# A two-layer graph transformer on one core: the same instruction steps in another written-out order

## The chip, the cores and the metric

The kernel runs on one core of one Trainium2 chip. The metric is the device time of one execution, in microseconds, as the median over runs. The engines are named as in the profile: PE is TensorE (PEld its weight loads), DVE is VectorE, ACT is ScalarE, POOL is GpSimd, SP is SyncE, whose queue issues nearly all DMAs.

## The reference, cut to what matters

Two layers run over 128 graphs of 128 nodes with 256 features, all in float32. `adj` is a 0/1 matrix per graph.

```python
# layer 0: attention over relations, then a feed-forward block
q, k = heads(src @ Wq + bq), heads(src @ Wk + bk)          # 8 heads of 32
attn = softmax(q @ k.T / sqrt(32))
out  = sum(attn * (adj == r) @ heads(src @ Wv[r] + bv[r]) for r in range(4))
x    = ln(src + out @ Wo + bo, g1, beta1)
x    = ln(x + gelu(x @ W1 + b1) @ W2 + b2, g2, beta2)      # 256 -> 1024 -> 256
# layer 1: two graph-attention steps, then a second feed-forward block
h = gat(gat(x, adj, W1, a1), adj, W2, a2)   # softmax over leaky_relu(Wh1 + Wh2.T) where adj > 0
h = ln(x + h, g_ln1, b_ln1)
return ln(h + relu(h @ w_ff1 + b_ff1) @ w_ff2 + b_ff2, g_ln2, b_ln2)
```

## The kernel before, in words

**Tiling.** The tokens are cut into 32 groups of four graphs (512 tokens). `fast_pass` (L190) carries each group through all stages; everything of three or four neighbouring groups runs interleaved. The weights stay in SBUF. A general path for other values of `adj` follows behind a flag and isn't run here.

**Stages.** Each stage is a Python generator, and each `yield` ends a step:

- `q`, `projected` (L744): q, k and v. The products of four blocks are made with seven half-size products instead of eight (a Strassen-Winograd form), in two PSUM banks (pqqa and pqqb, then pvqa and pvqb), with copies on ACT (L809, L806) and adds on DVE (L819, L831, L835, L804) between.
- `a`, `attention` (L959): for each pair p of graphs, scores `ps` on 32-row tiles of the array (L859), four exponentials `e` on ACT (L866), the mask on DVE (L875), then `pav` (L929) and `pden` (L917) on 32-column tiles, the normalisation (L941 to L956) and the output product `pwo` (L969).
- `d`, `folded` (L881): folds of e for the sums, four DMAs `es` by SP (L891), copies on ACT (L900), adds on DVE (L902).
- `f` and `fc`, `k` and `kc`: the two feed-forward blocks, both by `ffn` (L509). `f` and `k` are `others()` (L575), which works in the banks `ph1`/`po1` and `ph7`/`po7`; `fc` and `kc` are `chain()` (L619), which works in one bank, `seeded`. Here too seven half-size products replace eight. `product` (L521) issues two matmuls of 128x128 by 128x256, `product2` (L530) eight of 128x128 by 128x128.
- `l`, `layer1` (L1038): the two graph-attention steps, with `pw` (L1046), `py` (L1059) and `pg` (L1072), the spreading of a column over all partitions through HBM (two DMAs, L1008 and L1009) and `edges` (L1012) on ACT (L1017, L1023) and DVE.
- `n0` to `n3`, `norm` (L474): layer norms on DVE (L445), with the power -1/2 on POOL (L431); then the planes on ACT (L465) and a DMA transpose (L468). `t0` to `t2`, `turned` (L486): the copies of the transposed planes on ACT (L493), and the sums `yS` on DVE (L502 to L506).
- `in`, `rest`, `bo`, `out`, and the setup steps (`Lqk`, `wqk`, ...): loads, stores, prepared weights.

**The chain in `seeded`.** For each half r of a feed-forward block, `chain()` copies ph1 into `seeded` on ACT (L621, or L648 for the second half), adds the product T2 (yS), copies the bank out on ACT (L629, p16), adds the product T1, adds the bank to the hidden layer on DVE (L633), and adds the product B22. Each product on `seeded` waits for the step that read the bank before it.

**What sets the order.** Nothing is scheduled by the framework: engines take their instructions in the order in which Python issues them, and that order is written out in three strings, FRONT (L123), STEADY (L144) and TAIL (L159). `in_order` (L1163) reads tokens `name:group*times` and advances that stage's generator by one step each time; a group number is relative to the loop's. FRONT runs once, STEADY for g = 1 to 29, TAIL once. A step issues everything up to its next `yield`, on whichever engines it uses, DMAs on SP's queue included. Semaphore waits are added by the framework from the data that instructions share.

Of the kernel before, what the change touches and what calls it, by code (L numbers as in the profile page):

```python
# [120 lines left out]


FRONT = """  # L123
Lqk*2 in:0 q:0*2 L1 q:0 Lqk Lv Lqk wqk q:0*4 Lv q:0 a:0 Lv a:0*2 Lv L2 L1 a:0*2 rest:0 L1 Lv_ a:0
Lv_ L1 d:0*2 Lv_ q:0 a:0 q:0 w1 d:0*2 rest:0 L3 in:1 d:0*2 Lh1 Lo q:0*2 d:0 a:0 q:0 d:0 L1 q:0*2
a:0*2 q:0 a:0 wv a:0 w1 a:0*2 L1 a:0*6 d:0 bo:0 rest:1 d:0 w1 q:1*2 Lh1 d:0*2 q:1 Lg1 a:0 Lg1 L4
a:0 Lg1 q:1 d:0 bo:0 Lg1 q:1 d:0 q:1 Lg2 q:1 d:0 q:1 a:1 a:0 a:1 Lgat a:1 wqk d:0 a:1*2 a:0 a:1
a:0 d:1*2 a:1 a:0*4 Lgat L2 d:1 a:0*2 q:1 a:0 d:1*2 L3 q:1 a:0 b1 d:1 a:0 a:1 L2 bo:0 q:1 d:1
a:0*2 n0:0 q:1 b1 L2 n0:0 b1 output_bias q:1 d:1 a:1 n0:0*3 w2 n0:0 L4 b1 output_bias q:1 n0:0 w2
w1 Lgat a:1*2 Lh1 a:1 t0:0 gw f:0 a:1 b1 a:1 t0:0 Lgat a:1 q:1 t0:0*2 a:1 d:1 rest:1 a:1 fc:0 d:1  # L130
a:1 L4 t0:0 b1 d:1 f:0*2 q:1 t0:0 f:0 fc:0 a:1 d:1 L3 gw b1 a:1 fc:0 b1 f:0 fc:0 d:1 fc:0 d:1
a:1*2 f:0 L3 f:0 a:1 in:2 d:1*2 fc:0 a:1 f:0 w2 Lh1 w2 fc:0*2 gw f:0 fc:0*2 f:0 a:1*3 L3 fc:0*2
a:1 bo:1 fc:0 f:0 wv f:0 fc:0 f:0*2 fc:0 f:0 a:1 L4 fc:0*2 a:1*3 rest:2 u2 fc:0 a:1 fc:0 bo:1 a:1
f:0 fc:0 a:1 fc:0*2 f:0 a:1 f:0 fc:0 f:0 n0:1 Lg2 fc:0 n0:1 fc:0 n0:1*2 f:0 fc:0 n0:1 q:2 f:0 wqk
fc:0*2 q:2 L3 n0:1 fc:0 n0:1 f:0*2 gw t0:1 wqk fc:0 bo:1 f:0 fc:0 t0:1 gelu fc:0 n1:0 t0:1 n1:0
gw q:2*2 c1 q:2 t0:1 n1:0 c1 n1:0 f:1 q:2*2 n1:0 t0:1 q:2 t0:1 fc:1 n1:0 c1 n1:0 q:2*2 f:1 t1:0
q:2 fc:1 u2 t1:0 l:0 f:1 fc:1 l:0 t1:0 l:0 fc:1 t1:0 l:0 fc:1 l:0 u1 l:0*3 fc:1 f:1 l:0 f:1 q:2
f:1*2 fc:1 f:1 fc:1*2 q:2 f:1 fc:1*2 q:2*2 c1 exp q:2 wv fc:1 c1 q:2 c1 l:0*2 c1 l:0 fc:1 l:0*2
u2 q:2 l:0*2 fc:1 l:0 a:2 f:1 a:2*3 d:2 l:0 a:2 fc:1 l:0*2 a:2 l:0 d:2 l:0*3 u2 l:0 d:2 l:0*3 f:1
u1 q:2 l:0 u1 d:2 fc:1 f:1 Lh2 q:2 fc:1 q:2 f:1 a:2 f:1 q:2 Lh2 wv fc:1*2 f:1 u1 c1 d:2 f:1 l:0*2  # L140
fc:1 f:1 l:0*2 a:2 q:2 fc:1 l:0*2 fc:1 l:0*2 fc:1 l:0*3 f:1 q:2*2 d:2 fc:1 d:2 q:2 l:0 f:1 fc:1
l:0*3 q:2 l:0*2 n2:0 q:2 rest:2 f:1 fc:1 n2:0*2 q:2 n2:0*2 fc:1*3 d:2
"""
# [36 lines left out]


# [1352 lines left out]
```

## Time and profile before

| | before |
|---|---|
| median of 3 runs | 2634.33 us (2633.99 to 2634.73) |
| profiled execution | 2633.71 us |
| its span, first to last instruction | 2631.9 us |
| PE / PEld busy | 2598.8 / 2302.5 us |
| DVE / ACT / POOL busy | 2246.7 / 1857.4 / 141.8 us |
| mean granted PE clock | 0.998 |
| start of FFN1 of group 1 / 2 / 3 / 30 | 101.5 / 193.1 / 274.1 / 2440.6 us |
| most groups from there to the next | 80.13 us |

A line of the timeline has the start in us, the time in us, the engine, the line of the kernel, the operation, the tile written and those read, the shapes, and how many instructions were merged; in brackets is the idle time before it and what ended it. One float32 matmul shows as two passes on PE, each with a weight load on PEld, so a `product` is four records and a `product2` sixteen. Ends of matmuls are modelled, so the spacing of starts is what to read: 0.216 us from pass to pass of 256 columns, 0.112 us for 128 columns. With PE busy for 99% of the span, what can change without changing the work is in the spacings that are longer than these.

### The profile page before, as it was taken

What the parts mean: (1) busy time and instruction counts of PE and PEld (TensorE: products, weight loads), DVE (VectorE), ACT (ScalarE), POOL (GpSimd) and SP (SyncE); (2) the same over time, 40 slices, a digit from 0 to 9 for tenths busy, and PEclk for the clock granted to TensorE, in tenths of its full rate; (3) what the DMA queues carried; (4) which work ended last, traced back from release to release, by engine and by line L of the source; (5) the groups of instructions that cost most, each with busy time, mean ns of one, the idle gap of its engine ahead of it and who ended that gap; (6) DMA issues with size and microseconds to landing.
All of it is one profiled execution on the core that took longest, in us unless ns stands there. A gap on an engine that the chain in (4) does not pass through costs nothing.

```text
span 2631.9 us, 54467 instructions
## 1 busy us (share of the span) xinstructions
PE 2598.8 (99%) x20842; PEld 2302.5 (87%) x20842; DVE 2246.7 (85%) x5921; ACT 1857.4 (71%) x3839; POOL 141.8 (5%) x137
## 2 busy tenths in 40 slices
PE   8999999999999999999999999999999999999997
PEld 6888898888988988988889888889889899888886
DVE  5888888889888988888988888988889888889877
ACT  4767777667677677776776776776767777767764
POOL 0000000000000000000000000000000000000000
PEclk9999999999999999999999999999999999999999
DMA  6222232232233222222322232222323222222211
GB/s 177 69 63 61 64 66 66 53 73 65 55 67 61 65 61 65 65 66 53 75 64 59 63 67 59 63 64 65 69 53 73 61 61 65 65 57 70 60 29 34
DMA packets 317371, 170.60 MB, mean 65 GB/s; under 512 B 222768, under 2 KB 295600, under 8 KB 317104
## 3 DMA queue, kind: packets, MB, share of 16 engines
q1 hardware_dynamic: 316000, 166.66, 28.0%
q8 instruction: 166, 2.72, 0.4%
q14 instruction: 101, 0.83, 0.1%
q10 hardware_dynamic: 1104, 0.40, 0.1%
HBM read 66.20 MB, written 16.90 MB: 32 GB/s over the span
## 4 chain that ended last, share of the span: by engine, by line
PE 92%; DVE 3%; DMA 2%; ACT 2%; issue 1%; SPq 0%; POOL 0%; ACTq 0%; POOLq 0%; DVEq 0%
PE po L534 16%; PE ph L525 16%; PE seeded L525 13%; PE seeded L534 12%; PE pwo L969 4%; PE pav L929 4%; PE pw L1046 4%; PE pqqa L789 4%; PE pvqa L789 4%; PE pqqb L789 3%; PE pvqb L789 3%; PE ps L859 2%; PE py L1059 2%; PE pg L1072 2%; PE pden L917 1%; DVE x L445 1%
## 5 line engine op out<-in xcount | busy, mean ns | idle before, releaser
L465 ACT COPY planes<-x 128x512 uint16<-128x512 uint16 x384 | 227.0, 617 | 161.2 <-DVE x L445 160.5
L493 ACT COPY yT<-pT 128x512 uint16<-128x512 uint16 x384 | 268.0, 764 | 63.6 <-DMA pT<-planes 63.6
L431 POOL TENSOR_TENSOR rs<-rs,mhalf 128x4 f32<-128x4 f32 x129 | 139.5, 1081 | 2430.7 <-DVE rs L430 1836.9
L525 PE MATMUL seeded<-yS,w_L_gnn_w_ff 128*128 128x256 f32 x768 | 208.8, 394 | 2.8 <-ACT seeded L621 1.6
L866 ACT ACTIVATE e<-ps 128x512 f32<-128x512 f32 x256 | 137.0, 591 | 103.1 <-issue 89.9
L525 PE MATMUL seeded<-yS,w_L_gnn_W 128*128 128x256 f32 x768 | 204.0, 388 | 1.3 <-DVE yS L505 0.9
L525 PE MATMUL ph<-yT,w_L_gnn_w_ff 128*128 128x256 f32 x768 | 201.1, 385 | 0.5 <-ACT yT L493 0.2
L525 PE MATMUL ph<-yT,w_L_gnn_W 128*128 128x256 f32 x768 | 197.1, 380 | 0.0
L407 DVE BATCH_NORM_STATS2 st<-x 128x6 f32<-128x256 f32 x512 | 190.8, 414 | 2.4
L534 PE MATMUL po<-w_L_gnn_W,hT 128*128 128x128 f32 x1536 | 187.1, 275 | 0.5 <-ACT hT L549 0.5
L534 PEld LDWEIGHTS po<-w_L_gnn_W,hT 128*128 128x128 f32 x1536 | 184.0, 192 | 3.8 <-ACT hT L549 0.6
L534 PE MATMUL po<-w_L_gnn_w_ff,hT 128*128 128x128 f32 x1536 | 186.9, 275 | 0.0
L534 PEld LDWEIGHTS po<-w_L_gnn_w_ff,hT 128*128 128x128 f32 x1536 | 183.8, 192 | 3.4
L525 PEld LDWEIGHTS seeded<-yS,w_L_gnn_w_ff 128*128 128x128 f32 x768 | 135.7, 189 | 51.3 <-ACT p L629 16.1
L875 DVE TENSOR_TENSOR pm<-e,adj 128x512 f32<-128x512 f32 x256 | 169.7, 683 | 10.3 <-ACT e L866 9.2
L525 PEld LDWEIGHTS seeded<-yS,w_L_gnn_W 128*128 128x128 f32 x768 | 140.4, 190 | 35.2 <-ACT p L629 8.3
L633 DVE TENSOR_TENSOR hT<-seeded,p 128x512 f32<-128x512 f32 x128 | 87.6, 684 | 90.6 <-PE seeded L525 87.1
L525 PEld LDWEIGHTS ph<-yT,w_L_gnn_w_ff 128*128 128x128 f32 x768 | 143.7, 191 | 23.3 <-ACT seeded L648 0.6
L525 PEld LDWEIGHTS ph<-yT,w_L_gnn_W 128*128 128x128 f32 x768 | 143.3, 190 | 18.8 <-ACT seeded L621 0.4
L900 ACT COPY pm<-e 64x512 f32<-64x512 f32 x256 | 157.6, 616 | 2.3
L629 ACT COPY p<-seeded 128x512 f32<-128x512 f32 x128 | 75.0, 586 | 97.0 <-PE seeded L525 96.7
L549 ACT ACTIVATE hT<-hT,c_L_gnn_b_ff 128x256 f32<-128x256 f32 x256 | 112.4, 498 | 34.5 <-DVE hT L633 32.3
(195 smaller groups left out, 6399.2 us busy)
## 6 DMA issues: line engine op xcount, KB each, us to landing
es<-e SPq DMA_DIRECT2D x256, 128.0 KB, 2.4
xT<-in_xT_dram SPq DMA_DIRECT2D x32, 512.0 KB, 3.9
x<-in_x_dram SPq DMA_DIRECT2D x32, 512.0 KB, 3.9
out_dram<-x SPq DMA_DIRECT2D x31, 512.0 KB, 2.9
spread<-hbm SPq DMA_DIRECT2D x61, 256.0 KB, 4.1
adj<-in_adjT_dram SPq DMA_DIRECT2D x32, 256.0 KB, 4.4
pT<-planes SPq DMA_TRANSPOSE x192, 3.1
w_L_gnn_W<-in_L_gnn_W_dram SPq DMA_DIRECT2D x8, 256.0 KB, 5.1
```

What stands on the lines that cost most here:

```text
L407: nc.vector.bn_stats(st[:, b % 2, :], S["x"][:, b, :])
L431: nc.gpsimd.tensor_tensor(rs[:, bs], rs[:, bs], k.mhalf[:, bs], op=ALU.pow)
L465: nc.scalar.copy(planes[:, :, b], words)
L493: nc.scalar.copy(o.rearrange("p (b t h) -> p h b t", b=2, h=2), pT[:, :, :, c, :])
L525: nc.tensor.matmul(bank[:, s * TH : (s + 1) * TH], wa[:, form, 0, f * P : (f + 1) * P], m, start=start and s == 0, stop=True, skip_group_c ...
L534: nc.tensor.matmul(bank[:, s * P : (s + 1) * P], m[:, f, s * P : (s + 1) * P], wb_[:, form, f, :], start=start and s + f == 0, stop=True, ...
L549: nc.scalar.activation(o[:, s], o[:, s] if src is None else src[:, s * TH : (s + 1) * TH], func, bias=ba[:, f : f + 1],)
L789: nc.tensor.matmul(bank[:, s * TH : (s + 1) * TH], *ops, start=start and s == 0, stop=True, skip_group_check=True,)
L866: nc.scalar.activation(e[:, s], pss[s], AF.Exp, scale=SCALE)
L875: nc.vector.tensor_mul(pm[:, s], S["e", p][:, s], S["ad"][:, pair(p), None, :].to_broadcast([P, 2, NCH, P]),)
L900: nc.scalar.copy(ea[own], e[own, hs, lo].rearrange("p s c i -> p s (c i)"))
L929: nc.tensor.matmul(pav[s * DH : (s + 1) * DH, u, c, :], v[:, d0 : d0 + DH], m[:, s, u, c, :], start=(r == 0), stop=(r == 1),)
```

## The change

Only the three strings differ. The set of steps is the same (FRONT has 486 steps before and 526 after, STEADY 291 and 291, TAIL 449 and 409), every instruction of the old program is in the new one, and the order among the steps of a stage stays. What moves is the interleaving of stages on every engine, and where the period of STEADY is cut: its first step is `f:0` before and `k:-1` after. The string STEADY in full, of FRONT and TAIL their first and last lines:

```diff
 FRONT = """
-Lqk*2 in:0 q:0*2 L1 q:0 Lqk Lv Lqk wqk q:0*4 Lv q:0 a:0 Lv a:0*2 Lv L2 L1 a:0*2 rest:0 L1 Lv_ a:0
-Lv_ L1 d:0*2 Lv_ q:0 a:0 q:0 w1 d:0*2 rest:0 L3 in:1 d:0*2 Lh1 Lo q:0*2 d:0 a:0 q:0 d:0 L1 q:0*2
...
+Lg1 Lqk in:0 Lqk q:0 Lqk L1 q:0 Lqk q:0*4 rest:0 q:0 Lv*3 Lv_ q:0 a:0 L1 a:0*2 Lv a:0 L1 Lv_ a:0
+L1 Lg2 L1 d:0 Lv_ d:0 q:0 a:0 q:0*2 Lh1 d:0 a:0 d:0 q:0 d:0*2 L2 d:0 w1 a:0 d:0 a:0 q:0 w1 q:0*2
...
 STEADY = """
-f:0*2 a:1 f:0 q:1*3 n2:-1*2 t2:-1 fc:0 a:1 t2:-1*2 a:1*2 t2:-1 f:0 fc:0 k:-1 t2:-1 a:1 t2:-1 fc:0
-k:-1 a:1 kc:-1 a:1*3 n1:0 d:1 kc:-1*2 a:1 n1:0 d:1 k:-1 d:1 a:1 d:1 a:1*3 k:-1*2 kc:-1*2 d:1*3
-k:-1 n1:0 k:-1 a:1 d:1 n1:0 kc:-1 a:1 n1:0 k:-1 kc:-1 bo:1 kc:-1 k:-1*2 n1:0 a:1 k:-1 a:1*4
-kc:-1*4 n1:0 a:1*2 in:2 kc:-1 a:1 bo:1 kc:-1 k:-1 a:1 t1:0 k:-1 kc:-1 t1:0 k:-1 t1:0 a:1 kc:-1*2
-k:-1 l:0*2 kc:-1 l:0 t1:0 k:-1 l:0 a:1 l:0*2 a:1 kc:-1 l:0*2 n0:1 kc:-1 n0:1 bo:1 l:0 k:-1 kc:-1
-q:2 n0:1 kc:-1*2 n0:1 rest:2 k:-1 q:2 n0:1*2 l:0*2 kc:-1 l:0*2 k:-1*2 kc:-1 q:2 k:-1 q:2 kc:-1
-l:0 n0:1 l:0 kc:-1 q:2 gelu kc:-1*2 l:0 t0:1 l:0 k:-1 kc:-1 l:0 t0:1 l:0*2 t0:1 k:-1 t0:1 f:1 l:0
-kc:-1 l:0 t0:1*2 q:2*2 k:-1 q:2 l:0 fc:1 f:1 l:0 fc:1*2 kc:-1 f:1 l:0 f:1 q:2 l:0 q:2 n3:-1 fc:1
-l:0 f:1 l:0 f:1 fc:1 l:0 fc:1*2 f:1*2 fc:1*2 n3:-1 q:2 n3:-1 fc:1 f:1 fc:1*2 f:1 fc:1 out:-1
-f:1*2 fc:1 q:2 rest:2 f:1 fc:1*2 l:0 f:1 l:0 q:2 l:0 fc:1*2 l:0 q:2 f:1 q:2 fc:1 l:0 q:2 f:1 q:2
-fc:1*2 f:1 q:2 l:0 a:2 fc:1 l:0 a:2 l:0 f:1 a:2 exp q:2 l:0*2 a:2 l:0 a:2 fc:1 a:2 d:2 a:2 l:0
-q:2 f:1 d:2 l:0*3 d:2 q:2 d:2 l:0 fc:1 d:2 q:2 l:0 d:2 fc:1 a:2 q:2 d:2 n2:0 q:2 d:2 q:2 fc:1
-n2:0*2 q:2 n2:0 f:1 q:2 n2:0 q:2 fc:1 q:2 fc:1*2
+k:-1 a:1 k:-1 a:1 k:-1 kc:-1 a:1*2 d:1 k:-1 d:1 kc:-1 n1:0 d:1 k:-1 a:1 k:-1 d:1 n1:0 in:2 k:-1
+kc:-1*3 a:1*2 kc:-1 n1:0*2 kc:-1 a:1 bo:1 kc:-1 a:1*2 kc:-1 a:1 n1:0 a:1 k:-1 a:1*2 k:-1*2 t1:0
+k:-1 kc:-1 t1:0 bo:1 kc:-1 a:1*3 kc:-1 k:-1 t1:0 a:1 l:0 t1:0 l:0 bo:1 l:0*2 kc:-1 k:-1 l:0*3
+kc:-1*2 n0:1 l:0 n0:1*2 kc:-1*2 k:-1*2 l:0 n0:1*2 kc:-1*2 n0:1 kc:-1 n0:1 l:0 q:2*2 k:-1 kc:-1
+k:-1 l:0*2 q:2 kc:-1 q:2 l:0 k:-1 kc:-1 q:2 kc:-1 t0:1 l:0*2 kc:-1 k:-1 kc:-1 t0:1*2 l:0 t0:1 f:1
+l:0 q:2 l:0 kc:-1 l:0*2 k:-1 l:0 k:-1 kc:-1 t0:1 l:0*2 rest:2 fc:1 l:0 t0:1 q:2 l:0 fc:1 kc:-1
+l:0 f:1 fc:1 f:1 l:0*2 f:1 l:0 fc:1 f:1 q:2 f:1 fc:1*2 f:1 q:2 f:1 fc:1 n3:-1 fc:1 q:2*3 f:1*2
+n3:-1*2 fc:1*4 l:0*2 q:2 fc:1 f:1 l:0 fc:1 q:2 f:1*3 gelu out:-1 fc:1 f:1 fc:1 l:0*2 f:1 q:2 fc:1
+q:2*2 fc:1 q:2 fc:1*2 l:0 fc:1*2 l:0 f:1 a:2*3 l:0 a:2*2 l:0 d:2 f:1 l:0*2 f:1 q:2 a:2 d:2*2 a:2
+d:2 q:2 l:0 fc:1 l:0 d:2 l:0*3 fc:1 d:2 rest:2 q:2 fc:1 l:0 a:2 q:2 n2:0 d:2 q:2*2 d:2 fc:1 n2:0
+exp n2:0*5 q:2*3 t2:0 fc:1 q:2 f:1*2 fc:1 f:1 t2:0 fc:1 q:2 f:1 t2:0 a:2 q:2*2 t2:0 fc:1 q:2 a:2
+f:1 a:2*2 k:0 a:2*2 d:2 fc:1 a:2 kc:0 a:2 t2:0*2 fc:1 a:2 k:0 d:2 kc:0 n1:1 d:2 k:0 a:2 kc:0 d:2
+n1:1
 """
 TAIL = """
-n2:-1 bo:1 f:0 a:1 n2:-1 q:1 f:0 q:1*2 t2:-1 f:0 t2:-1*2 fc:0 a:1*2 t2:-1 f:0 fc:0*2 n1:0 a:1
...
-kc:1*3 k:1 kc:1*2 n3:0 kc:1*2 k:1*2 n3:0 kc:1*2 k:1*2 kc:1*3 out:-1 k:1*2 out:0 z:1 kc:1*2 z:1
-kc:1 z:1*2
+k:-1 a:1 k:-1 a:1*3 k:-1 d:1 kc:-1 d:1 k:-1 n1:0 kc:-1 d:1 a:1 n1:0 d:1 a:1 kc:-1 k:-1*3 kc:-1*2
...
+k:1*2 kc:1 checks kc:1*4 k:1 kc:1*2 k:1 kc:1*2 k:1*2 kc:1 k:1 kc:1*3 k:1 kc:1 out:0 k:1 z:1*2
+kc:1 z:1 kc:1 z:1
 """
```

On ACT, the order around the scores of pair 1 and FFN2 of the group two before reads, from the two programs (group 15 and 13): before `e, e, seeded (L621), e, e`, after `e, e, e, seeded (L621), e`.

## The prediction

> **What bounds the kernel now.** I read the page first (shares, then the chain that ended last), then the timeline of one steady period, then the timeline of the end.
>
> ```profile
> PE 2598.8 (99%) x20842; PEld 2302.5 (87%) x20842; DVE 2246.7 (85%) x5921; ACT 1857.4 (71%) x3839; POOL 141.8 (5%) x137
> ...
> PE 92%; DVE 3%; DMA 2%; ACT 2%; issue 1%; SPq 0%; POOL 0%; ACTq 0%; POOLq 0%; DVEq 0%
> ```
>
> TensorE sets the time, and its work (20842 passes) is the same after the change. So an order can win only what TensorE loses between passes. The steady 29 passes through STEADY repeat every 80.13 us (start of the first FFN1 product of one group to that of the next); a two-matmul product (four passes of 128x256) starts 0.864 us after the one before it when nothing is lost. I listed every start-to-start spacing above that. In the timeline from 1328 us:
>
> ```profile
> 1329.65 1.03 PE L525 MATMUL ph<-yS,w_L_gnn_W 128*128 128x256 f32 x4
> 1330.52 0.73 PEld L525 LDWEIGHTS seeded<-yS,w_L_gnn_W 128*128 128x128 f32 x4 [0.25 <-ACT seeded L648]
> 1330.53 1.13 PE L525 MATMUL seeded<-yS,w_L_gnn_W 128*128 128x256 f32 x4
> ...
> 1331.28 0.84 PEld L525 LDWEIGHTS ph<-yT,w_L_gnn_W 128*128 128x128 f32 x4
> 1331.49 1.03 PE L525 MATMUL ph<-yT,w_L_gnn_W 128*128 128x256 f32 x4
> ...
> 1331.75 0.59 ACT L629 COPY p<-seeded 128x512 f32<-128x512 f32 x1 [0.45 <-PE seeded L525]
> ...
> 1332.38 0.73 PEld L525 LDWEIGHTS seeded<-yS,w_L_gnn_W 128*128 128x128 f32 x4 [0.27 <-ACT p L629]
> ```
>
> The weight load of ph begins 0.21 us ahead of its matmul (1331.28, 1331.49), under the product before. That of seeded at 1330.52 sits behind a wait for ACT, and begins with its matmul: the product after it starts 0.96 us later, not 0.864. At 1332.38 the copy (1331.75 + 0.59) ends 0.02 us before TensorE is free, which looks free, and still costs 0.10 us. Matching every matmul that waits with the end of the ACT or DVE instruction it waits for gives the price: released over 0.18 us before TensorE is free, nothing; 0 to 0.08 us before, 0.104 us; later than that, the lateness + 0.06 + 0.104.
>
> A typical period loses 0.840 us at six such spots, all on `seeded`: 0.118 (1330.5), 0.134 (1332.4), 0.063 (1364.5), 0.134 (1366.4), 0.258 (1368.4), 0.133 (1377.2). Another 0.572 us goes at the six edges where TensorE passes between full products and the tiled ones (ps, pav, pden): 0.085, 0.101, 0.086, 0.104, 0.092, 0.104. At the end of the run one gap dominates:
>
> ```profile
> 2551.55 1.03 PE L525 MATMUL ph<-yT,w_L_gnn_w_ff 128*128 128x256 f32 x4
> 2556.03 2.02 PE L525 MATMUL ph<-yS,w_L_gnn_w_ff 128*128 128x256 f32 x4 [3.45 <-DVE yS L502]
> 2557.84 1.84 PE L525 MATMUL ph<-yT,w_L_gnn_w_ff 128*128 128x256 f32 x4
> 2559.52 1.03 PE L525 MATMUL seeded<-yS,w_L_gnn_w_ff 128*128 128x256 f32 x4
> ```
>
> After it, two products take 1.81 and 1.68 us instead of 0.864: some 2.0 us more lost, in eight to nine passes at half speed.
>
> **What the Trainium skill says.** "TensorE: Matmul & The Clock Gate", The mechanism: TensorE's queue can pull a weight load ahead of matmuls in flight; the trace agrees for loads without a wait (0.21 us ahead) and shows that a load behind an unfinished wait stays put. Same page, LDWEIGHTS (loading the stationary operand): P/1.2 ns, so 107 ns for 128 columns; the trace's exposed load is 104. Same page, What's actually happening: after an idle window of about 3.4 us the clock falls to half; here a 3.45 us gap is followed by passes of 427 ns instead of 216. Same page, Architectural detail: ACT and DVE are strict FIFO, so what stands ahead in their queues counts.
>
> **The change part by part.** The instructions are the same, in another order. Per pass of STEADY both have 291 steps.
>
> *Five spots go.* Before, a product on `seeded` and the next one on it have one other product between (0.864 us of cover). The copy L629 needs from the start of the last pass 0.471 us to begin, of which 0.255 lies after that pass's 0.216, then 0.586, then 0.18 ahead of TensorE: 1.02 us. One product is short, two (1.73) are enough. In the new order of TensorE the T2 and T1 products have two products between them in all four places, B22 after T1 has two or more, and T2 of FFN1's second half follows ph1, ph7 and a q product. With the durations of the profile I laid both orders of one period on a ruler (each engine's next instruction after its last and after what it waits for, TensorE never held back). On before this finds the same six spots with margins of 0.078, 0.023, 0.036, 0.023, -0.092 and 0.023 us. On the new order five are gone, with 0.35 us or more outside the stretch described next: 0.118+0.134+0.134+0.258+0.133 = 0.777 us less.
>
> *The sixth grows.* Both orders have ps of pair 1, ph1, ph7, then seeded, which waits for the copy L621.
>
> ```profile
> 1362.76 1.13 PE L525 MATMUL ph<-yT,w_L_gnn_w_ff 128*128 128x256 f32 x4
> 1362.89 1.08 ACT L866 ACTIVATE e<-ps 128x512 f32<-128x512 f32 x2 [3.26 <-issue]
> ...
> 1363.72 1.03 PE L525 MATMUL ph<-yS,w_L_gnn_w_ff 128*128 128x256 f32 x4
> 1363.92 0.57 ACT L621 COPY seeded<-ph 128x512 f32<-128x512 f32 x1
> ...
> 1364.41 1.09 ACT L866 ACTIVATE e<-ps 128x512 f32<-128x512 f32 x2
> ...
> 1364.54 0.73 PEld L525 LDWEIGHTS seeded<-yS,w_L_gnn_w_ff 128*128 128x128 f32 x4 [0.20 <-ACT seeded L621]
> ```
>
> ACT runs two exponentials, then the copy. The new order puts three ahead of it, one more by 0.50 us (1.09 less 0.59). The copy then ends at 1364.99 instead of 1364.49, TensorE is free at 1363.72 + 0.864 = 1364.58, so it is 0.41 + 0.06 + 0.104 = 0.57 us; the ruler says a margin of -0.466, so 0.63. I take 0.60, 0.54 more than the 0.063 now. Behind it wait ACT's fourth exponential and the copies L900. On the ruler three later waits in FFN2 are short too (-0.256 ph7 by L584, -0.334 ph1 by L549, -0.191 pav by L875): all are backlog of ACT and DVE, not of TensorE, so 0.60 us lost once covers them. The six edges stay (six tiled edges a period in both).
>
> Net 0.777 - 0.54 = 0.24 us a period, x29 = **7.0 us**. Bounds: 0.777 x 29 = 22.5 if the sixth doesn't grow; a loss in the rival below.
>
> *Late landings of spread.* A few periods of before are longer than 80.13; summed, 3.8 us. At 590 us the cause is spread landing after 5.3 us (median 4.1), which holds ACT at L1017. With 1.6 us added to it on the ruler, both orders fall short, before by up to 0.12 us at three spots, the new one nowhere below 0.04. SP has the same DMAs in slightly other places (x load behind the es copies, adj behind both transposes); the ruler shows no wait on these. I take half: **1.9 us** (0 to 3.8).
>
> *Front.* The load order changes (a row of layer norm 1 first, xT ahead of the second part of Wq and Wk, Wv later), and 40 more steps move into FRONT, 40 fewer in TAIL. On the ruler the largest shortfall of TensorE in the first 240 us is 3.9 us before and 2.8 after: **1.1 us**. I don't know how the loads share the queues in the new order: -4 (loss) to +4.
>
> *Tail.* Same measure: the section at 2485 us, where TensorE loses 1.78 us before, falls short by 1.8 and now 0.5; the largest shortfall from 2550 us on is 6.1 before and 4.5 now, and it builds up in steps of at most 1.5 us, so no gap should reach 3.4 us and the half-speed passes (2.0 us) go. 1.3 + 1.5 + 2.0 = 4.8. The last chain:
>
> ```profile
> 2620.86 0.42 DVE L667 TENSOR_TENSOR x<-seeded,x 128x256 f32<-128x256 f32 x1
> 2621.20 0.87 DVE L445 SCALAR_TENSOR_TENSOR x<-x,mv,r_L_gnn_g_ln 128x256 f32<-128x256 f32 x2
> 2621.99 0.74 DVE L407 BATCH_NORM_STATS2 st<-x 128x6 f32<-128x256 f32 x2
> ...
> 2622.86 0.85 DVE L445 SCALAR_TENSOR_TENSOR x<-x,rs,r_L_gnn_b_ln 128x256 f32<-128x256 f32 x2
> ```
>
> DVE does a pair of affine passes (0.79 us) between the last add and its statistics; the new order does them ahead of the add: 0.7. Tail **5.5 us** (1 to 9).
>
> **Sum** against the profiled execution (2633.71; span 2631.9 and 1.8 around it): 7.0 + 1.9 + 1.1 + 5.5 = 15.5, so 2618.2. The median of the runs is 0.6 above the profiled one: **2618.8 us**.
>
> **Rivals.** *Deeper (15%):* the third exponential doesn't delay TensorE, 0.60 x 29 = 17.4 more: 2601.4. For: the order's maker would have avoided a stall in every period. Against: exponentials at 0.50 us each in a FIFO leave no room. *Same (9%):* the change doesn't do what it says: the spot at L621 takes 0.80 (net 0), spread and front give nothing or -2, the tail loses its gap but grows others: 2630 to 2637. For: the tail's waits are as many as before. *Slower (8%):* the four shortfalls of FFN2 don't share one stall but add, each chain restarting from TensorE after the stall: (0.466+0.256+0.334+0.191) + 4 x 0.164 = 1.90 us in place of 0.84, so 1.06 x 29 = 30.8 lost, less 8.5 from the other terms: 2656.6. It decides once that stretch loses over 0.84 + 8.5/29 = 1.13 us. Against: L584 copies a bank filled before the stall.
>
> **How the numbers follow.** Main case 68%, with its parts from 2610 to 2628. Range 2600 to 2630: it leaves out the slower case (0.08), half of the same (0.05) and what goes below 2600 (0.06). A measurement of this kernel can tell about 0.2% (5.3 us) from no change: faster 0.83, same 0.09, slower 0.08.
>
> **What would show it.** Period 79.9 us; no 0.104 at L629, L648 or L633 of the steady stretch; one stall of about 0.6 us before seeded in FFN2, released by L621; no passes of 427 ns past 2500 us; span near 2616. Wrong if the period is above 80.1, if two or more of L621, L584, L549, L875 hold TensorE in each period, or if the front moves by over 4 us.

## The result and the profile after

| | before | after |
|---|---|---|
| median of 8 runs each | 2634.53 us | 2626.25 us (2624.99 to 2627.67) |
| ratio | | 0.9969, 95% interval 0.9958 to 0.9979 |
| profiled execution / its span | 2633.71 / 2631.9 us | 2625.64 / 2623.5 us |
| start of FFN1 of group 3 / 30 | 274.07 / 2440.63 us | 273.84 / 2432.52 us |
| most groups from there to the next | 80.13 us | 79.81 us |

The kernel gains 8.3 us, half of the 15.5 that were forecast. The first part of the page, and its shares of the chain that ended last:

```profile
PE 2584.5 (99%) x20842; PEld 2310.1 (88%) x20842; DVE 2241.1 (85%) x5921; ACT 1854.2 (71%) x3839; POOL 149.7 (6%) x137
...
PE 86%; issue 4%; ACT 3%; DVE 3%; DMA 1%; POOL 0%; SPq 0%; DVEq 0%; ACTq 0%; POOLq 0%
```

The same passes take the time; only what lies between them changed. PE's share of the chain is smaller than before (92%) although TensorE loses less. At the stall shown below the chain leaves TensorE and goes back through the copy L621 to the exponentials and to the 3.80 us for which ACT was idle ahead of them, which count as "issue" (4%, 1% before). So these shares don't say what is lost. The costliest groups of the page name the place (the columns after the bar: busy us and mean ns, idle us before, and the releaser that ended most of it):

```profile
L525 PEld LDWEIGHTS seeded<-yS,w_L_gnn_w_ff 128*128 128x128 f32 x768 | 142.8, 190 | 41.6 <-ACT seeded L621 19.1
...
L525 PEld LDWEIGHTS seeded<-yS,w_L_gnn_W 128*128 128x128 f32 x768 | 144.9, 190 | 22.5 <-ACT p L629 1.0
```

In FFN1 (`w_L_gnn_W`) the largest share that one releaser has in the idle time ahead of the weight loads on `seeded` is 1.0 us in the whole run, and it was 8.3 us before (L629 both times). In FFN2 (`w_L_gnn_w_ff`) 19.1 us stand against L621, and 19.1 / 29 = 0.66 us a period. The timeline of a steady period shows it:

```profile
1279.74 1.57 ACT L866 ACTIVATE e<-ps 128x512 f32<-128x512 f32 x3 [3.80 <-issue]
1280.57 1.03 PE L525 MATMUL ph<-yS,w_L_gnn_w_ff 128*128 128x256 f32 x4
1281.19 0.62 ACT L621 COPY seeded<-ph 128x512 f32<-128x512 f32 x1
1281.71 0.62 ACT L866 ACTIVATE e<-ps 128x512 f32<-128x512 f32 x1
1281.86 0.73 PEld L525 LDWEIGHTS seeded<-yS,w_L_gnn_w_ff 128*128 128x128 f32 x4 [0.66 <-ACT seeded L621]
1281.86 1.13 PE L525 MATMUL seeded<-yS,w_L_gnn_w_ff 128*128 128x256 f32 x4 [0.26 <-ACT seeded L621]
...
1282.70 0.59 ACT L584 COPY p<-ph 128x512 f32<-128x512 f32 x1
1282.83 1.89 PE L525 MATMUL ph<-yT,w_L_gnn_w_ff 128*128 128x256 f32 x8
```

Three exponentials stand ahead of the copy. It ends at 1281.81; TensorE was free at 1280.57 + 0.864 = 1281.43. The product on `seeded` starts at 1281.86, 0.43 us late, and its weight load, which starts with it, costs 0.10 more: the spacing to the product after it is 1282.83 - 1281.86 = 0.97. Together 0.527 us. After that the products follow each other without a loss up to pav: the copy L584 at 1282.70 holds nothing.

In FFN1 the weight loads on `seeded` now start ahead of their matmuls, so nothing waits:

```profile
1328.07 0.84 PEld L525 LDWEIGHTS seeded<-yS,w_L_gnn_W 128*128 128x128 f32 x4
1328.28 1.03 PE L525 MATMUL seeded<-yS,w_L_gnn_W 128*128 128x256 f32 x4
1329.14 1.89 PE L525 MATMUL ph<-yT,w_L_gnn_W 128*128 128x256 f32 x8
```

The load at 1328.07 leads its matmul by 0.21 us, and there are two products (the x8 on ph) before the next on `seeded`. At the end of the run the 3.45 us wait is gone, and there are shorter ones:

```profile
2544.15 1.03 PE L525 MATMUL ph<-yT,w_L_gnn_w_ff 128*128 128x256 f32 x4
2546.45 1.10 PE L525 MATMUL ph<-yS,w_L_gnn_w_ff 128*128 128x256 f32 x4 [1.28 <-DVE yS L502]
2547.39 1.03 PE L525 MATMUL ph<-yT,w_L_gnn_w_ff 128*128 128x256 f32 x4
2549.54 1.13 PE L525 MATMUL ph<-yT,w_L_gnn_w_ff 128*128 128x256 f32 x4 [1.12 <-ACT p L584]
2550.51 1.03 PE L525 MATMUL seeded<-yS,w_L_gnn_w_ff 128*128 128x256 f32 x4
2552.26 1.13 PE L525 MATMUL seeded<-yS,w_L_gnn_w_ff 128*128 128x256 f32 x4 [0.73 <-ACT p L629]
```

Spacings of 2.30, 2.15 and 1.75 us in place of 0.864: 1.44, 1.28 and 0.89 lost. The granted clock of 2540 to 2560 us is 1.00.

**Where the 8.4 us of the two spans lie.** From group 3 to group 30 the run is 7.9 us shorter (2166.56 and 2158.68). 27 periods x 0.32 would be 8.6; the difference lies in periods longer than the usual one, which add 3.0 us in these 27 before and 3.8 after. Behind the mark of group 30 the new order still has 1.79 us more of TensorE's work to do (16 passes of 0.112 us), and ahead of group 3 so much less. Allowing for that, the tail gains 2.1 us and the front loses 1.6. 7.9 + 2.1 - 1.6 = 8.4.

### The profile page after: what moved, and what is told of

Read it like the earlier page. It is cut to its first block, busy times and chain, and to the rows that moved or that the text cites. A ratio compares the mean times of both kernels' runs of the same rounds, so it can differ in the third digit from the quotient of the medians.

```text
span 2623.5 us, 54324 instructions
## 1 busy us (share of the span) xinstructions
PE 2584.5 (99%) x20842; PEld 2310.1 (88%) x20842; DVE 2241.1 (85%) x5921; ACT 1854.2 (71%) x3839; POOL 149.7 (6%) x137
## 4 chain that ended last, share of the span: by engine, by line
PE 86%; issue 4%; ACT 3%; DVE 3%; DMA 1%; POOL 0%; SPq 0%; DVEq 0%; ACTq 0%; POOLq 0%
PE po L534 17%; PE ph L525 14%; PE seeded L525 12%; PE seeded L534 12%; PE pwo L969 4%; PE pw L1046 4%; PE pqqa L789 4%; PE pvqa L789 4%; PE pqqb L789 3%; PE pvqb L789 3%; PE pav L929 3%; PE py L1059 2%; PE pg L1072 2%; ACT e L866 1%; PE ps L859 1%
## 5 line engine op out<-in xcount | busy, mean ns | idle before, releaser
L431 POOL TENSOR_TENSOR rs<-rs,mhalf 128x4 f32<-128x4 f32 x129 | 146.9, 1139 | 2419.7 <-DVE rs L430 2409.3
L525 PE MATMUL seeded<-yS,w_L_gnn_w_ff 128*128 128x256 f32 x768 | 200.9, 384 | 9.2 <-ACT seeded L621 7.6
L525 PE MATMUL seeded<-yS,w_L_gnn_W 128*128 128x256 f32 x768 | 198.2, 380 | 0.7 <-ACT seeded L648 0.4
L525 PE MATMUL ph<-yT,w_L_gnn_w_ff 128*128 128x256 f32 x768 | 191.3, 384 | 1.5 <-ACT p L584 1.1
L525 PEld LDWEIGHTS seeded<-yS,w_L_gnn_w_ff 128*128 128x128 f32 x768 | 142.8, 190 | 41.6 <-ACT seeded L621 19.1
L875 DVE TENSOR_TENSOR pm<-e,adj 128x512 f32<-128x512 f32 x256 | 169.3, 681 | 3.4 <-ACT e L866 2.2
L900 ACT COPY pm<-e 64x512 f32<-64x512 f32 x256 | 157.4, 615 | 2.7
L445 DVE SCALAR_TENSOR_TENSOR x<-x,rs,r_L_gnn_b_ln 128x256 f32<-128x256 f32 x256 | 112.2, 479 | 18.6 <-POOL rs L431 15.3
L534 PEld LDWEIGHTS seeded<-w_L_gnn_W,hT 128*128 128x128 f32 x1024 | 124.1, 192 | 3.8 <-DVE x L655 0.5
L445 DVE SCALAR_TENSOR_TENSOR x<-x,rs,r_L_gnn_beta 128x256 f32<-128x256 f32 x256 | 112.1, 479 | 15.3 <-POOL rs L431 15.1
```

The lines of the kernel that those rows point to most:

```text
L431: nc.gpsimd.tensor_tensor(rs[:, bs], rs[:, bs], k.mhalf[:, bs], op=ALU.pow)
L445: nc.vector.scalar_tensor_tensor(x[:, b, :], x[:, b, :], mv[:, b, 0:1] if first else rs[:, b : b + 1], g if first else be, op0=ALU.subtrac ...
L525: nc.tensor.matmul(bank[:, s * TH : (s + 1) * TH], wa[:, form, 0, f * P : (f + 1) * P], m, start=start and s == 0, stop=True, skip_group_c ...
L534: nc.tensor.matmul(bank[:, s * P : (s + 1) * P], m[:, f, s * P : (s + 1) * P], wb_[:, form, f, :], start=start and s + f == 0, stop=True, ...
L875: nc.vector.tensor_mul(pm[:, s], S["e", p][:, s], S["ad"][:, pair(p), None, :].to_broadcast([P, 2, NCH, P]),)
L900: nc.scalar.copy(ea[own], e[own, hs, lo].rearrange("p s c i -> p s (c i)"))
```

## The experiments

"The new order" is the changed kernel. Each ratio is to the kernel before on the same chip. The first four runs were made on one chip, relief, cover2, front_b and tail_b on a second, resort and cover2_tail on a third, and the last two on a fourth; across chips it is ratios and periods that are compared. The period is the usual start-to-start spacing of groups; it repeats to 0.01 us within a run, so it resolves what a median of whole runs can't.

| run | median us | ratio (95%) | period us |
|---|---|---|---|
| copy3 | 2625.93 | 0.9971 (0.9959 to 0.9983) | 79.83 |
| copy5 | 2633.82 | 0.9999 (0.9991 to 1.0008) | 80.19 |
| cover3 | 2633.96 | 1.0003 (0.9995 to 1.0012) | 80.12 |
| exp3 | 2618.12 | 0.9941 (0.9928 to 0.9955) | 79.46 |
| relief | 2636.51 | 1.0016 (1.0009 to 1.0023) | 80.23 |
| cover2 | 2626.32 | 0.9977 (0.9968 to 0.9986) | 79.88 |
| front_b | 2622.05 | 0.9959 (0.9946 to 0.9973) | 79.80 |
| tail_b | 2627.24 | 0.9978 (0.9969 to 0.9987) | 79.82 |
| resort | 2624.61 | 0.9970 (0.9958 to 0.9982) | 79.85 |
| cover2_tail | 2624.56 | 0.9963 (0.9949 to 0.9976) | 79.88 |
| new_again | 2625.00 | 0.9970 (0.9958 to 0.9982) | 79.80 |
| front_b_again | 2622.21 | 0.9956 (0.9942 to 0.9970) | 79.81 |

### The copy L621 ahead of the third exponential (copy3)

The new order with one token of STEADY moved:

```diff
-f:1 a:2*2 k:0 a:2*2 d:2 fc:1 a:2 kc:0 a:2 t2:0*2 fc:1 a:2 k:0
+f:1 a:2*2 k:0 a:2*2 d:2 fc:1 kc:0 a:2*2 t2:0*2 fc:1 a:2 k:0
```

> The new order with the copy L621 moved one place forward on ACT in STEADY, ahead of the third exponential, as before the change; TensorE's order stays. Backlog theory (the copy is only the first of several waits behind a full ACT queue): seeded at L621 is nearly on time (0.06 to 0.10 us lost instead of 0.53), but the product on ph7 then waits for L584, late by about 0.25 us, and after it ph1 for L549; the period loses 0.42 to 0.52 in that stretch, so the time is 2623 to 2627. Place theory (what costs is the place of the copy behind the third exponential): 0.46 us a period is won, 29 x 0.46 = 13.4, so 2612.9. Adding theory (each late wait costs for itself): 0.07 + 0.42 + 0.50 + 0.35 = 1.34 us a period, 2650.

The time is within the range of the backlog theory. The stall at L621 shrinks to 0.063 us, and two others come up behind it:

```profile
1282.63 0.73 PEld L525 LDWEIGHTS seeded<-yS,w_L_gnn_w_ff 128*128 128x128 f32 x4 [0.20 <-ACT seeded L621]
...
1284.60 0.73 PEld L525 LDWEIGHTS ph<-yT,w_L_gnn_w_ff 128*128 128x128 f32 x4 [0.38 <-ACT p L584]
...
1286.59 0.73 PEld L525 LDWEIGHTS ph<-yT,w_L_gnn_w_ff 128*128 128x128 f32 x4 [0.40 <-ACT hT L549]
```

By spacings 0.141 + 0.104 at L584 and 0.155 + 0.104 at L549; with the 0.063, 0.567 us in all where the new order has 0.527. The period is the same to 0.02 us. So the loss isn't that of the place where L621 stands. It fits a backlog of ACT and DVE that TensorE pays for once, at whichever products the late releases fall.

### The copy behind all four exponentials (copy5)

```diff
 ...
-d:2 fc:1 a:2 kc:0 a:2 t2:0*2
+d:2 fc:1 a:2*2 kc:0 t2:0*2
 ...
```

> The new order with the copy L621 one place further back on ACT in STEADY, behind all four exponentials. If the stall is the time that ACT's queue needs up to the copy, it grows by one exponential (0.50 us) a period: 29 x 0.50 = 14.5, so 2640.8, and the stall before seeded is 1.03 us. If the stall is set by something else (the release of the bank, or the waits after it), it stays at 0.53 and the time within 2 us of 2626.

```profile
1286.57 0.73 PEld L525 LDWEIGHTS seeded<-yS,w_L_gnn_w_ff 128*128 128x128 f32 x4 [1.15 <-ACT seeded L621]
```

The load waits 1.15 us (0.66 in the new order): 0.49 more, one exponential in ACT's queue, as forecast (a stall of 1.02 us by spacings). The period grows by only 0.38, since pav, later by then, meets its operands without waiting and its stretch is 0.09 shorter, so the time stays under the 2640.8 that were forecast. One exponential more ahead of this copy gives back all of the 0.32 us that the change gains in a period.

### Three of the five spots covered in the kernel before (cover3)

The order before, with T1 of FFN2's second half put behind ph7 (first part of the diff) and steps of q moved between those of `fc` in FFN1's second half (the rest), so that two products lie between those on `seeded`. It is the diff's third part that cover2, below, does without (lines cut to the tokens that move):

```diff
-k:-1 kc:-1 t1:0 k:-1 t1:0 a:1 kc:-1*2
+k:-1 t1:0 k:-1 kc:-1*2 t1:0 a:1 kc:-1
...
-n3:-1 q:2 n3:-1 fc:1 f:1 fc:1*2 f:1 fc:1 out:-1
+n3:-1*2 fc:1 f:1 fc:1*2 f:1 q:2 fc:1 out:-1
...
-f:1*2 fc:1 q:2 rest:2 f:1 fc:1*2 l:0 f:1 l:0 q:2 l:0 fc:1*2 l:0 q:2 f:1 q:2 fc:1 l:0 q:2 f:1 q:2
+f:1*2 fc:1 q:2 rest:2 f:1 l:0 f:1 fc:1*2 l:0 q:2 l:0 fc:1 l:0 q:2 f:1 q:2 fc:1*2 l:0 q:2*3 f:1
```

> The order before, with three of its five spots covered by a second product and nothing else moved but what hangs on them: in FFN1's second half the products T2 and T1 on seeded, in FFN2's second half T1. If each spot costs what the trace of before shows (0.118 + 0.134 + 0.133 = 0.385 us a period), it wins 29 x 0.385 = 11.2 us: 2623.3, with a period of 79.75. If these small delays are made up elsewhere in the period (TensorE would have waited later anyway), it wins under 3 us: 2631.5 to 2634.5.

Nothing is won in time. The three spots go (0.385 us), and a new stall takes their place (the timeline around it, ACT and PEld):

```profile
1338.36 1.28 ACT L1023 ACT_TABLE_LOAD   x1
1339.66 0.63 ACT L1023 ACTIVATE gs<-gs 128x512 f32<-128x512 f32 x1
...
1341.24 1.05 ACT L866 ACTIVATE e<-ps 128x512 f32<-128x512 f32 x2
...
1342.52 1.16 PEld L1072 LDWEIGHTS pg<-yh,gs 128*128 128x128 f32 x6 [0.51 <-ACT e L866]
```

The moves changed ACT's order too: activations that came earlier now end later, with them the table load of L1023 (1.28 us, in line with everything on ACT) and the exponentials of pair 0, and pg needs a PSUM bank that these read. In the kernel before the last of them ended 0.56 us ahead of pg (at 1342.85, pg at 1343.41); that was all the cover there was. It costs 0.305 + 0.075. So the three spots were worth what was forecast, and another loss of the same size came up, which the forecast of "made up elsewhere" had not named. A step is not a product: its ACT part moves along.

### Two spots covered, ACT's order kept (cover2)

The first two parts of the diff above, which leave ACT's order as it was.

> The order before, with two of its five spots covered (a q product put ahead of T2 in FFN1's second half; T1 behind ph7 in FFN2's second half) and ACT's order kept: in cover3 the exponentials of pair 0 came later for pg, because the activations that ACT runs ahead of its table load had been moved back. If each spot costs what the trace of before shows and pg's slack of about 0.5 us is left alone, 0.118 + 0.133 = 0.251 us a period is won: 29 x 0.251 = 7.3, so 2626.4, with a period of 79.88. If TensorE waits later for what was won, as in cover3: 2632 to 2634.5, and a stall shows at another product.

The period comes out as worked out to 0.01 us. This confirms the price of a late release (0.104 us each while TensorE is otherwise full), and that it is paid in each of 29 periods. The median hits 2626.4 in part by luck: the gain is 6.1 us (0.0023 of 2632.42, with 0.0014 and 0.0032 as the ends of the interval) where 7.3 was worked out, and the kernel before was faster on this chip than on the one of the forecast. Three steps moved (one of q, two of `kc`) win three quarters of what the whole new order does.

### The third exponential left out (exp3)

On top of copy3 (this kernel leaves out an exponential that the result needs):

```diff
-            nc.scalar.activation(e[:, s], pss[s], AF.Exp, scale=SCALE)
+            nc.gpsimd.memset(e[:, s], 1.0) if p and s == 2 and 1 < S["g"] < 31 else nc.scalar.activation(e[:, s], pss[s], AF.Exp, scale=SCALE)
```

> As copy3, but the third exponential of pair 1 is left out for groups 2 to 30 (that quarter of e is set to one by GpSimd), so ACT has 0.50 us less to do in this stretch and TensorE the same. Backlog theory: with the queue half a microsecond shorter no wait after L621 is late any more; the stretch loses 0.06 to 0.2 us instead of 0.53, 29 x 0.33 to 0.47 = 10 to 13.5 us less than the new order: 2612.7 to 2616.5. Place theory: the same 2612.9 as its value for copy3, so the two runs differ by under 1 us. If the four waits are set by DVE or the transfers, not ACT: no gain, 2623 to 2627.

```profile
1281.78 0.73 PEld L525 LDWEIGHTS seeded<-yS,w_L_gnn_w_ff 128*128 128x128 f32 x4 [0.20 <-ACT seeded L621]
1282.53 1.49 PEld L525 LDWEIGHTS ph<-yT,w_L_gnn_w_ff 128*128 128x128 f32 x7
```

No product loses more than 0.02 us beyond the 0.064 at L621, where copy3 has two such losses. With 0.5 us of work less on ACT the period is 0.37 us shorter than copy3's (79.83). The rest reappears at pav, whose stretch is 0.11 us longer (2.56 and 2.45). So the amount of ACT's work in this stretch costs time, where its order doesn't. The median is above the 2612.7 to 2616.5 of the backlog theory: less is won than the queue was shortened by.

### One copy handed to DVE (relief)

The new order with L621 as in copy3, L584 and L629 ahead of the first L900, the affine passes of layer norm 1 moved behind the mask products, and one of the copies L900 made by DVE, ahead of the adds L902 and L592:

```diff
-                    nc.scalar.copy(ea[own], e[own, hs, lo].rearrange("p s c i -> p s (c i)"))
+                    (nc.vector.tensor_copy if p and lo and h == 0 else nc.scalar.copy)(ea[own], e[own, hs, lo].rearrange("p s c i -> p s (c i)"))
```

> The new order with ACT's queue in the stretch from the exponentials of pair 1 to pav shortened and re-sorted: L621 ahead of the third exponential, L584 and L629 ahead of the first L900 copy, one of the four L900 copies of pair 1 done by DVE, and DVE's first affine passes of layer norm 1 behind the two mask products. TensorE's order and work stay. Backlog theory: 0.06 us is lost at L621 and nothing at L584, L549 and pav, 0.46 us a period less, 29 x 0.46 = 13.3: about 2613, with a period of 79.3 to 79.4. If DVE, which takes the copy, becomes the bound: pav waits for L875 by 0.3 us or more and the gain is under 5 us, 2621 to 2626.

```profile
1287.39 0.42 DVE L900 COPY pm<-e 64x512 f32<-64x512 f32 x1
1287.90 0.69 DVE L902 TENSOR_TENSOR es<-es,pm 128x512 f32<-128x512 f32 x1
1288.51 0.68 DVE L592 TENSOR_TENSOR hT<-ph,p 128x512 f32<-128x512 f32 x1
...
1289.25 0.73 PEld L525 LDWEIGHTS ph<-yS,w_L_gnn_w_ff 128*128 128x128 f32 x4 [0.76 <-DVE hT L592]
```

The add L592, which empties the bank of ph, stands behind the copy and the add L902. Its product waits 0.516 + 0.104 us, pav's stretch grows by 0.3, and DVE has no idle time between 1281 and 1294 us. The kernel is slower than before, and slower than either theory had it. DVE holds TensorE, as the second theory said, but at L592 and not at the mask product L875, and the time lies 10 us above its range. Part of that is a queue position (L902 ahead of L592), so the next run takes the position apart from the amount.

### The same order with ACT's work left on ACT (resort)

L900 stays on ACT, L592 goes ahead of L902, one fold is put behind L549. Against relief, at the head of STEADY (lines cut; the first steps of TAIL change alike, and L900 is as in the new order):

```diff
-k:-1 a:1 k:-1 a:1 k:-1 kc:-1 a:1*2 n1:0 d:1*2 k:-1 d:1 kc:-1 d:1 n1:0
+k:-1 a:1 k:-1 d:1 a:1 k:-1 kc:-1 a:1*2 n1:0 k:-1 d:1*2 kc:-1 d:1 n1:0
 ...
```

> As relief, but without the work moved to DVE: the L900 copy stays with ACT (behind L549), and DVE does the add L592, for which the next product on ph7 waits, ahead of L902. In relief DVE had no idle time between 1281 and 1294 us and reached L592 late by 0.52 us because L900 (0.35) and L902 (0.60) stood ahead of it. DVE theory (the stretch is bound by ACT and DVE alike, and DVE has half a microsecond of slack in the new order only because TensorE waits for L621): no stall at L592, 0.06 at L621, and pav waits for the last L875 by 0.2 to 0.4 us; the period is 79.55 to 79.75 and the time 2 to 7 us under the new order, 2619 to 2624. If DVE is late for another reason than what stands ahead of L592: the stall at L592 stays near 0.5 us and the time is 2634 or more.

```profile
1278.33 0.73 PEld L525 LDWEIGHTS seeded<-yS,w_L_gnn_w_ff 128*128 128x128 f32 x4 [0.20 <-ACT seeded L621]
...
1284.65 0.69 DVE L875 TENSOR_TENSOR pm<-e,adj 128x512 f32<-128x512 f32 x1
1284.70 0.23 PEld L929 LDWEIGHTS pav<-pm,v 128*32 128x32 f32 x6
1285.46 0.14 PEld L929 LDWEIGHTS pav<-pm,v 128*32 128x32 f32 x2 [0.52 <-ACT planes L465]
```

The products have no stall but the 0.064 at L621, and the stall at L592 is gone as the position theory says. Yet the period is 79.85. pav now waits 0.555 us inside, till the mask product ends at 1285.34 (the bracket names ACT's planes; the release that came last before 1285.46 is DVE's L875). Three orders of the same work give 79.81, 79.83 and 79.85 with the loss at L621, at L584 and L549, and at pav. The forecast of this run (79.55 to 79.75) was wrong, and the half microsecond belongs to the stretch from ps to pav, not to a place in it. Whether ACT's or DVE's share of it sets the sum was not taken apart by a run: taking 0.5 us from ACT won 0.37, giving 0.42 to DVE lost 0.4. The traces point to DVE as the fuller of the two. From the last pass of ps to the first of pwo it is busy for 10.90 of 11.16 us in the new order (ACT 10.44), for 10.85 of 11.11 before the change, for 11.36 of 11.60 in relief and for 10.72 of 10.82 in exp3.

### The old front on the new order (front_b, new_again, front_b_again)

front_b has the new order with FRONT's steps sorted as before:

```diff
-Lg1 Lqk in:0 Lqk q:0 Lqk L1 q:0 Lqk q:0*4 rest:0 q:0 Lv*3 Lv_ q:0 a:0 L1 a:0*2 Lv a:0 L1 Lv_ a:0
+Lqk*2 in:0 q:0*2 L1 q:0 Lqk Lv Lqk wqk q:0*4 Lv q:0 a:0 Lv a:0*2 Lv L2 L1 a:0*2 rest:0 L1 Lv_ a:0
...
```

> The new order, with the steps of FRONT sorted as they came before the change (the loads too); STEADY and TAIL are the new ones. If the order of FRONT is what made the first groups late, with passes at half speed at 31 and 62 us, the third group's first FFN1 product comes 1.6 us or more earlier (272.2 instead of 273.84), no pass runs at half speed there, and the time is 1.6 to 2.7 us less: 2623.6 to 2624.7. If the lateness comes with having 40 steps more in FRONT, whatever their order, it stays: 2626.

It is the fastest version that does the whole work, so it was run once more, beside the new order on the same chip. Its group 3 starts at 271.69 us, earlier than forecast, but not for the reason given: passes ran at half speed in it too, from 30.6 us on.

> The new order itself, on the same chip as front_b_again and its runs of the kernel before. Half-speed passes near 31 us appeared in one trace with the new FRONT and not in another (tail_b), and in front_b too: if they come by chance and not with the order, this trace may lack them, and its third group then starts at 272.1 to 272.5 instead of 273.84. The ratio to before should be 0.997 again (8 us).

> The new order with FRONT's steps sorted as before the change, beside the new order on one chip. If FRONT's old order is worth something (first product on pq at 7.66 instead of 8.0 to 8.3 us, no half-speed passes near 62 us), it is 1 to 3 us faster than new_again. If the gain of front_b over the new order came from comparing different chips: within 0.5 us of new_again.

Again 2622.21 against 2625.00: the old front is 2.8 us better than the new one, though one of the new order's six times (2621.41) lies among those of the old front. Both beat the kernel before. In the profiled executions group 3 starts at 271.66 (new_again) and at 270.91 (front_b_again), which is 0.75 of the 1.9 us between their spans; 0.31 lies between groups 3 and 30, and 0.88 behind them, where new_again has a stall of 1.0 us at 2463 us that the new order's first execution hasn't. The loads explain little of it: the first product pq starts at 7.56 to 8.33 us in the eight traces with the new front and at 7.59 to 8.06 in the six with the old one.

The profiled executions of one kernel differ by as much. In the new order's first one the product pq took

```profile
31.14 5.40 PE L719 MATMUL pq<-xT,w_qk 128*128 128x512 f32 x8 [1.64 <-ACT e L866]
```

and in front_b_again

```profile
31.55 3.70 PE L719 MATMUL pq<-xT,w_qk 128*128 128x512 f32 x8 [1.70 <-ACT e L866]
```

The idle time ahead is the same, and the passes take 1.70 us more in the first. The new order's view by windows, for the same execution, shows why (its columns: window, its length, then PE, PEld, DVE, ACT and POOL busy, the granted PE clock, the DMA share and GB/s):

```profile
31.00:36.00 5.00, 4.86 (x8) 2.07 (x9) 1.63 (x3) 2.04 (x5) 0.00 (x0) 0.66 0.75 170
60.00:66.00 6.00, 5.75 (x25) 4.70 (x25) 5.06 (x20) 4.37 (x9) 0.90 (x1) 0.72 0.50 131
```

A granted clock of 0.66 over 5 us is half speed for 3.4 us, 1.7 us lost, and 0.72 over 6 us the same again. Group 3 of the first profiled execution stands 2.2 us later than in new_again, whose clock falls once, at 60.8 us. With this STEADY it starts at 273.84 us with two such stretches, at 271.66, 272.12 (tail_b) and 271.69 (front_b) with one, and at 270.91 (front_b_again) with none: with one stretch each the two fronts are about even, and what differs is how many there are. One begins between 57 and 69 us in seven of the eight traces with the new front and in one of the six with the old. There the new front puts sixteen passes of one column in a row (L345, the steps `b1`), behind scores on 32 rows:

```profile
57.45 1.15 PE L859 MATMUL ps<-qT,kT 32*128 32x128 f32 x26 [0.15 <-DVE v L738]
59.43 0.60 PE L345 MATMUL pbias<-temp,w_L_gnn_W 128*128 128x1 f32 x4 [0.83 <-ACT e L866]
60.29 1.50 PE L345 MATMUL pbias<-temp,w_L_gnn_W 128*128 128x1 f32 x12 [0.25 <-DVE c_L_gnn_b L349]
```

The clock falls at 62.34. In the kernel before, these passes come four or eight at a time between products of 256 columns, and the clock stays. This is read from the traces (the last section has the count); no run moved the `b1` steps alone.

### The old tail on the new order, the new tail on the old (tail_b, cover2_tail)

tail_b has the new order up to group 29 and then the remaining steps in the order before; cover2_tail is cover2 with the new order of the tail. Of the second:

```diff
 TAIL = """
-n2:-1 bo:1 f:0 a:1 n2:-1 q:1 f:0 q:1*2 t2:-1 f:0 t2:-1*2 fc:0 a:1*2 t2:-1 f:0 fc:0*2 n1:0 a:1
+n2:-1*2 t2:-1 f:0*2 t2:-1 f:0 t2:-1 a:1 q:1*2 t2:-1 fc:0 q:1 a:1 f:0 a:1*2 k:-1 a:1*2 d:1 fc:0
...
```

> The new order up to group 29, and from there the steps that are left in the order before. If the traces are read rightly, the tail's order is worth about 2.1 us: 2628.4. If the tail was worth the 5.5 us of the prediction (and something else in the new order lost the difference): 2631.8. In both the gap of over 3 us at 2550 us and the half-speed passes after it come back. If the tail's order is worth nothing: 2626.

> cover2 with the steps after group 29 in the new order. tail_b took 3.2 us longer from the first FFN1 product of group 29 to the last product than the new order; if the tail's order alone is worth that, this run is 3.2 us faster than cover2, 2623.1, with the period of cover2 (79.88) and without the 3.6 us gap at 2545 us. If the new tail is only good behind the new STEADY: within 1 us of cover2, 2626.3.

With the old tail the gap and the half speed come back on the new order:

```profile
2546.09 1.03 PE L525 MATMUL ph<-yT,w_L_gnn_w_ff 128*128 128x256 f32 x4
2550.57 1.10 PE L525 MATMUL ph<-yS,w_L_gnn_w_ff 128*128 128x256 f32 x4 [3.45 <-DVE yS L502]
2551.51 1.72 PE L525 MATMUL ph<-yT,w_L_gnn_w_ff 128*128 128x256 f32 x4
2553.02 1.91 PE L525 MATMUL seeded<-yS,w_L_gnn_w_ff 128*128 128x256 f32 x4
```

tail_b's median is 1.2 us under the 2628.4 that the traces had given, and cover2_tail's 1.5 above its 2623.1. From the start of group 30 to the end tail_b takes 193.9 us, the new order 191.0 and 191.75 in its two profiled executions: its tail is worth 2.1 to 2.9 us. On the old order the same tail is worth 2.45 us (271.46 to 269.01 from group 29 on). The whole runs were made on different chips; the ratios to the kernel before, 0.9977 and 0.9963, have intervals of 0.001 to either side and can't sharpen this. In all four traces with the old tail (before, cover2, cover3, tail_b) the clock falls once behind the gap; in the ten with the new tail it never does there.

## Why the prediction was right, and where it was off

**Five spots, 0.777 us a period: right.** All five are gone. cover2 shows the price by itself for two of them, with the old order for everything else.

**The sixth spot at L621, 0.60 us: right in place and kind, 0.07 too large.** It has 0.423 + 0.104 = 0.527. The net is therefore 0.777 - (0.527 - 0.063) = 0.313 where 0.24 was taken; measured 0.32. In the sum, 29 x 0.32 = 9.3 in place of 7.0.

**"0.60 us lost once covers them": right.** The three later shortfalls don't show in the new order, and copy3 and resort show what they come to: the same half microsecond at another place. This rules out the slower rival (adding, 2656.6), which copy3 tested directly, since there each chain restarts from TensorE with the stall in front removed. It also rules out that the deeper rival could be had by a better place for L621: with the copy in its old place, copy3 runs at 79.83.

**Late landings of spread, 1.9 us: wrong, it is nothing.** Over the 28 spacings from group 2 on, the longer periods add 3.8 us before and 3.9 after. The failing step is the one that took half of 3.8 because the ruler showed no shortfall with a late spread: the new order has these periods as well. In its first execution spread lands after 5.3 us too, issued at 585.1, ACT waits 5.50 us for it at L1017, and that period is 80.77 us: 0.41 is lost ahead of py and 0.54 ahead of a product on `seeded`, where the ruler left 0.04 us to spare. Periods that grew for other reasons were not traced one by one.

**Front, 1.1 us: wrong in sign.** With the phase of the mark allowed for, it is 1.6 us later in the first profiled execution and 0.6 earlier in the second, and the runs with the old front are 2.8 us faster as a whole. The ruler counted shortfalls of TensorE only; what it had no way to count is stretches at half clock (1.7 us each when TensorE is busy), of which the new front has more. It is within the -4 to +4 that was given.

**Tail, 5.5 us: the mechanism right, the size off by half (2.1 to 2.9).** The long gap and its half clock went, as told, and the loss of 1.78 us at 2485 us fell to 0.42 (with 0.89 more at 2492 us in the first execution, none there in the second). The failing step is to count the largest shortfall, "6.1 before and 4.5 now", as 1.5 us of gain with the steps of the build-up free of charge: the gap turned into losses of 1.44, 1.28 and 0.89 us in a row, where before only one product paid (3.61), and there is one more of 1.07 us at 2563 us. A loss of 1.39 at 2573 us (pg behind L1035) has its like in one of 1.21 before (py behind L1035), and 0.41 + 0.83 at 2594 to 2596 us became 0.37. The prediction also took a gap of 3.4 us as what brings half clock; that none came is right for the tail, but at 31 us a gap of 1.64 brought it. And the last chain gives nothing instead of 0.7, since only one pair of affine passes moved ahead of the add, and the add then stands behind it in DVE's queue:

```profile
2611.99 0.88 DVE L445 SCALAR_TENSOR_TENSOR x<-x,mv,r_L_gnn_g_ln 128x256 f32<-128x256 f32 x2
2612.78 0.42 DVE L667 TENSOR_TENSOR x<-seeded,x 128x256 f32<-128x256 f32 x1
2613.11 0.87 DVE L445 SCALAR_TENSOR_TENSOR x<-x,rs,r_L_gnn_b_ln 128x256 f32<-128x256 f32 x2
2613.90 0.75 DVE L407 BATCH_NORM_STATS2 st<-x 128x6 f32<-128x256 f32 x2
```

The product was done at 2612.16; the add starts at 2612.78, 0.62 us later. From there to the last matmul (`pflag`, L1200) it is 0.64 us shorter than before.

**Sum.** 15.5 was 7.0 + 1.9 + 1.1 + 5.5. Measured between the two profiled executions it is 8.6 for 27 periods, -0.8 in the longer ones, -1.6 in front and 2.1 in the tail (in these two the few periods outside groups 3 to 30), 8.4 in all. So the period gave more than was forecast, and of the 8.5 us forecast outside it next to nothing came. That the time is still within the range owes something to the width of the range: the two terms with a count of instructions behind them (five spots, one stall) were good to 0.1 us a period; the three that rested on the difference of two largest shortfalls, or on "half of it", were not.

## What to carry to other kernels

A product that follows its own drain too closely costs its weight load even when the release comes just in time; with two products between, it cost nothing here, and moving three steps won most of what a complete new order did. Before moving a stalled copy in an engine's queue, add up the work of that engine, and of the engines that it hands on to, between the two products that enclose it: if there is too much of it for the time, the stall moves to the next consumer and only work taken out shortens it. A step that is moved for its matmuls moves its ACT and DVE work too, so look what stood within half a microsecond behind it.

## What the runs showed of the hardware

- In resort the load of 32 columns that waits inside pav starts 0.12 us after the mask product ends (1285.34, 1285.46); the loads of 128 columns on `seeded` start 0.05 us after their copy (1281.81, 1281.86). pav's stretch is 2.98 us there and 2.45 in the new order.
- The half clock comes in stretches of 3.41 us, or of two or three of them in a row (6.83 in copy3, 10.24 in exp3), at times that are not tied to the program. In the record of the granted clock they start at 31.62 and 62.34 us in the new order's first profiled execution, 30.72 us apart, which is nine times 3.413; in two other runs with two such stretches the distance is the same 30.72. A gap of 1.64 to 1.70 us ahead of pq brought half speed in some executions and not in others of the same kernel. This agrees with the Trainium skill, "TensorE: Matmul & The Clock Gate", What's actually happening, where the activity window is 3.413 us and free-running. It doesn't take a window without any pass, though: in the new order's first execution TensorE ran passes of ps from 28.27 to 29.50 us and pq from 31.14, within the window ahead of the slow one (28.20 to 31.62).
- What it takes can be worked out from the traces. Lay windows of 3.413 us through the starts of the stretches, and in each add up the passes at 0.216 us for 256 columns (fewer in proportion), times the part of the 128 x 128 array that they use, so that a pass on 32 rows counts a quarter and one of a single column next to nothing. Over all 14 traces, from 6 us on, 30 windows at full clock are filled to 0.39 or less, and each is followed by half clock (14 of them where TensorE's work ends); 10658 are filled to 0.40 or more, and none is. The two ahead of the stretches above have 0.38 and 0.18, though PE shows as busy for much of the second. The emptiest window of front_b_again's front has 0.42; the gap of the old tail leaves 0.01 to 0.36, the tail of the new order no window under 0.50. This count was made after the runs, and no run put it to the test.
